# A two-layer post-norm decoder on one core: first scan and constants moved into the schedules, and VectorE steps given to other engines

## The chip, the core and the metric

The kernel runs on one core of a Trainium2 chip. TensorE (PE), VectorE (DVE), ScalarE (ACT) and GpSimd (POOL) each work through their own queue in order; SyncE (SP) issues most of the DMAs, in order too, and GpSimd issues the indirect ones. The metric is device time of one execution in microseconds.

## The reference

A batch of 64 sequences of 128 tokens, width 128, float32, goes through two layers of three blocks; after every block comes `x = layernorm(x + block(x))`.

- Layer 0: a linear attention (`rms_norm`, q/k/v, `exp(k)` with running sums over the tokens, a gated output), a cross-attention with 16 heads of 8 over a context of 77 tokens with a bias and a mask, and a mixture of experts (two shared ones, and the best 2 of 8 for each token).
- Layer 1: a selective scan, `h = exp(delta*A)*h + delta*u*B; y = h.C + u*D`, with 16 states for each of 256 channels, behind a causal convolution of width 4; a cross-attention with 16 heads of 64; and a feed-forward block with ternary weights and activations rounded to 8 bits:

```python
def _bitlinear(x, w):
    return jnp.einsum('bsi,oi->bso', _act_quant(x), _weight_quant(w))
gate = jax.nn.silu(_bitlinear(x, w_gate))
up = _bitlinear(x, w_up)
return _bitlinear(gate * up, w_down)
```

## The kernel before, in words

**Tiling.** The sequences are cut into 16 groups (`g`) of four (`b`). A tile of one group is 128 partitions by 4 x 128 floats. Routed experts work on chunks (`ch`) of two groups: their rows are sent by GpSimd with indirect DMAs into a buffer in DRAM (`rows_in`, zeroed beforehand by `c_fill`, L845 to L857), sorted by expert, worked on in 15 tiles of 256 rows (`c_tile`) and fetched back with indirect DMAs (`c_get`, L417, mixed into the residual at L406).

**Order of the work.** Each layer is one hand-written schedule, the class `Flow` (from L67). Threads (Python generators) yield steps; a step names its engine, a cost, what it depends on and the buffer slots it takes. `Flow.run` takes, again and again, the step that can start first by these costs, with `ahead` as a handicap or bonus for a thread, `table` for ScalarE's function table (a switch is counted as 1.3 us) and `port` for steps that must not overlap with one another on the port which DVE and POOL share. The outcome is a fixed order of instructions in each engine's queue; `Wait` only orders the plan, and on the chip an instruction waits for the data and the buffers it uses. `flow.run(16)` plans layer 0 with up to 16 groups open, `flow.run(5)` layer 1 with five. Expert tiles of the last four chunks are placed in layer 1, beside the scan.

**Layer 0** (L433 to L1069). Per group: `a_head`, `a_seq`, `a_tail` (linear attention), `b_load`, `b_head`, `b_seq`, `b_tail` (cross-attention; the row-maximum subtraction L785 runs on POOL; `b_load` adds the mask to the bias on POOL at L684), `c_route`, `c_rank`, `c_send`, `c_shared`. Weights that belong to layer 1 are collected in `later` by `reserve` and loaded through SP by the thread `weights(later)`, added at group 4; x is loaded group by group at L543, and fills are issued as soon as x of an early group was requested.

**Layer norm** (`norm`, L255 to L279). For each sequence of the group DVE runs `bn_stats` and `bn_aggr` (L261, L262); POOL then turns mean and variance into scale and shift in four small instructions (L269 to L272); ACT applies them (L278). There are seven norms per group (lnA, lnB, lnC, ln1 to ln4). The first block's `rms` (L527 to L536) uses `bn_aggr` too.

**Between the layers** (L1070 to L1145). Layer 0's buffers are given back. Then, outside of any schedule: `negA`, the convolution's taps (loaded and multiplied by `W_in`), its edge and bias constants, the four weights `yWq`, `yWk`, `yWv`, `yWo` of the cross-attention and its folded output bias, and the ternary weights of the feed-forward block. Only then does `Flow` plan layer 1.

**Layer 1.** `scan_inputs(g)` (L1205 to L1300): load x from DRAM (`mid`), transpose, the convolution (L1230, with its edge at L1233), Silu on ACT, the projection (L1253), which goes to DRAM (`rows`) to be broadcast, and delta = softplus(...) on PE (L1268), ACT (abs at L1278), DVE (maximum at L1282, a correction at L1294) and three POOL passes (L1297 to L1299). `spread(g)` fetches the rows of B and C, broadcast over the partitions, two states at a time; `decays(g)` computes dA on ACT (L1359); `states(g)` multiplies du and B on DVE (L1375) and runs the scan on DVE (L1383); `outputs(g)` multiplies h and C on POOL (L1407) and sums over states on PE with identity matmuls into `acc` (L1420). A group has 16 such steps. Then come `gates`, ln1, the cross-attention (`cross_inputs`, `values`, `attend`), ln2, ln3, and `feed(g)`, which rounds the activations, multiplies by the ternary weights and forms `silu(gate)*up` with a Tanh on ACT (L1758) and two DVE steps (L1762, L1766), then a scale per row (L1772 to L1774), a rounding on DVE (L1777) and ACT (L1783), and the product with the last weights (L1799).

## Time and profile before

| | |
|---|---|
| runs, us | 3307.13, 3314.45, 3314.62 |
| profiled execution, us | 3323.51 |
| its span, us | 3321.7 |
| granted TensorE clock, mean | 0.941 |
| PE busy | 2867.3 us, 86% |
| DVE busy | 2616.4 us, 79% |
| ACT busy | 2097.9 us, 63% |
| POOL busy | 1741.2 us, 52% |
| DMA | 438.23 MB, mean 132 GB/s |

The span reaches from the first to the last instruction of the profiled execution; device time has 1.8 us around it. "Busy" is the time in which an engine works on an instruction of its own. A group of the profile is all instructions of one line with one shape: line, engine, operation, output <- inputs, shapes, count, then busy us and mean ns, and idle time of the engine ahead of them with what ended most of it. Line numbers in the views of this kernel are those of the listing above.

### The profile page before, as it was taken

To read this page: it belongs to the slowest core of one execution; us is meant where nothing else is said; L and a number is where in the kernel's file an instruction comes from. 1 tells how busy PE (TensorE), PEld (TensorE's weight loads), DVE (VectorE), ACT (ScalarE), POOL (GpSimd) and SP (SyncE) were. 2 spreads that over 40 slices of the span, in tenths; PEclk is the share of its full clock that TensorE was granted. 3 is DMA by queue.
4 is the path that set the end of the run, shared out by engine and by line. 5 is a ranking of instruction groups with operands and counts; after the bars stand their busy time and mean duration, and the time that the engine had idled before them with its cause. 6 is when DMAs were issued, how large, how long until landed. Compare 5 with 4: busy or idle time off the path is not lost. (4 is left out here: it accounts for less than half of the span.)

```text
span 3321.7 us, 55836 instructions
## 1 busy us (share of the span) xinstructions
PE 2867.3 (86%) x19880; PEld 1937.7 (58%) x19880; DVE 2616.4 (79%) x5007; ACT 2097.9 (63%) x3831; POOL 1741.2 (52%) x1603
## 2 busy tenths in 40 slices
PE   3989999999996679889898988888899988888883
PEld 2667777776864346556464655555665655656462
DVE  3777787888754488878987888888888898879864
ACT  1655767667731566767666766666677767767653
POOL 3454564655454356445745556664645556554531
PEclk7899999999998899999998999999999999999986
DMA  5134252333223464365545554464536533333400
GB/s 152 46 95 123 71 142 71 108 105 85 67 82 117 140 232 151 128 189 172 188 149 179 178 180 166 147 213 154 173 118 196 173 119 127 116 121 122 154 23 7
DMA packets 256542, 438.23 MB, mean 132 GB/s; under 512 B 40683, under 2 KB 155014, under 8 KB 256262
## 3 DMA queue, kind: packets, MB, share of 16 engines
q1 hardware_dynamic: 248070, 417.86, 39.9%
q0 software_dynamic: 8192, 16.79, 1.6%
q8 instruction: 157, 2.57, 0.3%
q14 instruction: 123, 1.01, 0.1%
HBM read 376.37 MB, written 58.20 MB: 131 GB/s over the span
## 5 line engine op out<-in xcount | busy, mean ns | idle before, releaser
L1407 POOL TENSOR_TENSOR h<-h,C 128x1024 f32<-128x1024 f32 x256 | 604.6, 2363 | 571.4 <-DVE bu L1375 365.5
L1420 PE MATMUL acc<-h,ident 128*128 128x512 f32 x1024 | 540.1, 653 | 138.5 <-POOL h L1407 137.5
L1383 DVE TENSOR_TENSOR_SCAN h<-dA,bu 128x1024 f32<-128x1024 f32 x256 | 583.8, 2280 | 26.7 <-PE acc L1420 7.7
L1375 DVE TENSOR_TENSOR bu<-du,B 128x1024 f32<-128x1024 f32 x256 | 355.8, 1390 | 79.2 <-DMA B<-rows 77.2
L1420 PEld LDWEIGHTS acc<-h,ident 128*128 128x128 f32 x1024 | 187.2, 201 | 346.5 <-POOL h L1407 193.5
L1359 ACT ACTIVATE dA<-delta,negA 128x508 f32<-128x508 f32 x512 | 336.4, 714 | 57.2 <-DVE h L1383 56.7
L349 PE MATMUL mm<-t_rT,t_we 128*128 128x256 f32 x960 | 250.8, 394 | 14.9 <-DMA t_we<-in_we 6.7
L1609 POOL TENSOR_TENSOR s<-s,rs 128x1232 f32<-128x1232 f32 x64 | 145.6, 2276 | 175.7 <-DVE rs L1603 111.6
L349 PEld LDWEIGHTS mm<-t_rT,t_we 128*128 128x128 f32 x960 | 175.9, 194 | 76.5 <-issue 22.6
L785 POOL TENSOR_TENSOR s<-s,mx 128x1232 f32<-128x1232 f32 x64 | 144.0, 2255 | 143.9 <-DVE mx L782 69.5
L1509 PE MATMUL mm<-xT,w_yWq 128*128 128x256 f32 x512 | 165.6, 406 | 21.4 <-ACT kT L1502 8.9
L1627 ACT COPY pT<-mm 77x512 f32<-77x512 f32 x256 | 136.4, 583 | 55.9 <-PE mm L1616 53.9
L1498 ACT ACTIVATE qT<-mm,w_ybq 128x256 f32<-128x256 f32 x256 | 122.4, 478 | 68.7 <-PE mm L1510 67.8
L793 ACT COPY pT<-mm 77x512 f32<-77x512 f32 x256 | 132.7, 586 | 50.8 <-PE mm L800 45.1
L1566 PEld LDWEIGHTS mm<-kT,qT 64*128 64x128 f32 x2048 | 130.3, 194 | 51.3 <-issue 18.6
L1616 PE MATMUL mm<-ident,s 128*77 128x128 f32 x1024 | 140.9, 283 | 19.7 <-POOL s L1609 10.6
L977 POOL DMA_INDIRECT rows_in<-cx,pos x128 | 124.3, 971 | 57.9 <-DVE pos L957 24.9
L800 PE MATMUL mm<-ident,s 128*77 128x128 f32 x1024 | 139.3, 290 | 17.1 <-ACT s L787 12.4
L417 POOL DMA_INDIRECT t_got<-rows_out,pos x128 | 131.2, 1025 | 40.6 <-issue 28.5
L1616 PEld LDWEIGHTS mm<-ident,s 128*77 128x77 f32 x1024 | 118.9, 152 | 54.8 <-POOL s L1609 21.8
L1566 PE MATMUL mm<-kT,qT 64*128 64x77 f32 x2048 | 148.0, 286 | 0.9 <-DVE s L1592 0.4
L374 PEld LDWEIGHTS mm<-t_we,t_th 128*128 128x128 f32 x960 | 123.6, 197 | 32.8 <-issue 15.1
(335 smaller groups left out, 7025.5 us busy)
## 6 DMA issues: line engine op xcount, KB each, us to landing
B<-rows SPq DMA_DIRECT2D x256, 512.0 KB, 4.9
C<-rows SPq DMA_DIRECT2D x256, 512.0 KB, 4.0
t_we<-in_we SPq DMA_DIRECT2D x120, 384.0 KB, 3.6
rows_in<-zero SPq DMA_DIRECT2D x8, 1920.0 KB
t_row<-rows_in SPq DMA_DIRECT2D x120, 128.0 KB, 3.2
rows_out<-t_yo SPq DMA_DIRECT2D x120, 128.0 KB, 3.6
cg<-in_ctxT SPq DMA_DIRECT2D x32, 154.0 KB, 4.4
x<-in_x SPq DMA_DIRECT2D x16, 256.0 KB, 4.2
```

The lines of the kernel that those rows point to most:

```text
L349: mm(o[:, c * TR : (c + 1) * TR], we.tile[:, n * 256 + c * P : n * 256 + (c + 1) * P], rT.tile, start=True, stop=True,)
L785: lambda: pool.tensor_tensor(s, s, mx.tile.unsqueeze(2).to_broadcast([P, NH, M]), ALU.subtract), port=True,
L800: nc.tensor.transpose(pt[0:M, i * P : (i + 1) * P], s[:, 4 * q + i, :], ident)
L1359: act(dA[:, j, :, 1:], delta[:, c, :, 1:], AF.Exp, scale=negA[:, c, n + j : n + j + 1])
L1375: order[g, c, n] = dve.tensor_tensor(bu, du[:, c, :].unsqueeze(1).to_broadcast([P, 2, W]), BC["B", g, c, n], ALU.mult)
L1383: dve.tensor_tensor_scan(h.rearrange("p n s -> p (n s)"), DA[g, c, n].rearrange("p n b s -> p (n b s)"), bu.tile.rearrange("p n s -> p (n ...
L1407: one = pool.tensor_tensor(h, h, BC["C", g, c, n], ALU.mult)
L1420: mm(acc, ident, HS[g, c, n][:, j, :], start=n + j == 0, stop=n + j == NS - 1)
L1509: mm(pk[:, 0 : 2 * P], yWq[:, cs], xT.tile[:, pair * 2 * P : (pair + 1) * 2 * P], start=True, stop=True)
L1566: mm(sc[:, i * M : (i + 1) * M], qT[r, i, b2 * P : (b2 + 1) * P], kT[r, i, b2 * M : (b2 + 1) * M], start=True, stop=True,)
L1609: lambda: pool.tensor_tensor(s, s, rs.tile.unsqueeze(2).to_broadcast([P, NH, M]), ALU.mult), port=True,
L1616: nc.tensor.transpose(pt[0:M, i * P : (i + 1) * P], s[:, 4 * q + i, :], ident)
```

## The change

The diff, cut to what acts; `...` marks what is left out. The line numbers of the changed kernel differ from those above.

In the common part, ahead of layer 0, room is made that outlives layer 0, and `norm` skips `bn_aggr`, whose work POOL does from the two halves that `bn_stats` gives:

```diff
+    magic = new(const, [P, 1], "magic")
+    pool.memset(magic, MAGIC)
...
+    negA, conv_all = new(const, [P, 2, NS], "negA"), new(const, [P, 2], "conv_all")
+    taps, first = new(const, [P, 4, 256], "taps"), new(const, [3, 256], "first")
+
+    iT0 = new(const, [P, G, P + 3], "iT0")
+    pool.memset(iT0[:, :, 0:3], 0.0)
+    u0, delta0, du0 = (new(const, [P, 2, W], n) for n in ("u0", "delta0", "du0"))
+    sl_rows = Slots([new(dram, [3 * NS, W], f"rows{i}", bufs=1) for i in range(2)])
...
-            dve.bn_stats(st[:, b, :], v[:, b, :])
-            dve.bn_aggr(mv[:, b, :], st[:, b, :])
...
-            yield flow.dve(0.55, key + ("st", b), deps, lambda: stats(b))
+            yield flow.dve(0.3, key + ("st", b), deps, lambda: dve.bn_stats(st[:, b, :], v[:, b, :]))
...
-            pool.tensor_scalar(r, mv[:, :, 1], LN_EPS, None, ALU.add)
-            pool.tensor_scalar(sh, mv[:, :, 0], -1.0, None, ALU.mult)
+            pool.tensor_tensor(d, st[:, :, 1], st[:, :, 4], ALU.subtract)
+            pool.tensor_tensor(r, st[:, :, 2], st[:, :, 5], ALU.add)
+            pool.tensor_tensor(sh, st[:, :, 1], st[:, :, 4], ALU.add)
+            pool.tensor_tensor(d, d, d, ALU.mult)
+            pool.tensor_scalar(r, r, 1.0 / P, LN_EPS, ALU.mult, ALU.add)
+            pool.tensor_scalar(d, d, 0.25, None, ALU.mult)
+            pool.tensor_scalar(sh, sh, -0.5, None, ALU.mult)
+            pool.tensor_tensor(r, r, d, ALU.add)
             pool.tensor_tensor(r, r, mhalf[:, :G], ALU.pow)
             pool.tensor_tensor(sh, sh, r, ALU.mult)
-        yield flow.pool(2.0, key + ("r",), [key + ("st", b) for b in range(G)], steps)
+        yield flow.pool(3.3, key + ("r",), [key + ("st", b) for b in range(G)], steps)
```

Indirect DMAs are planned as users of the shared port, and a mix waits, in the plan, for both loads of its pair:

```diff
-            yield S.flow.dve(0.7, k + ("mix", b), [k + ("got", b), k + ("v",)], add)
+            yield S.flow.dve(0.7, k + ("mix", b), [k + ("got", b | 1), k + ("v",)], add)
...
-            (got,) = yield S.flow.pool(2.0, k + ("got", b), out, get, S.got, landing=3.0)
+            (got,) = yield S.flow.pool(2.0, k + ("got", b), out, get, S.got, landing=3.0, port=True)
...
-                yield POOL(1.0, ("send", g, b, i), [...], send, landing=3.0)
+                yield POOL(1.0, ("send", g, b, i), [...], send, landing=3.0, port=True)
```

In layer 0: x of group 0 is loaded second; fills and `later` wait for a first layer norm in the plan; slots are fewer; the scan's constants and `scan_inputs(0)` (the same steps as before, with the maximum on ACT) are threads of layer 0:

```diff
     w_qkv = load(w0, "w_qkv", [P, 384])
+    x0 = new(w0, [P, G, P], "x0")
+    nc.sync.dma_start(out=x0, in_=tokens(t["x"], 0))
     w_swiglu = load(w0, "w_swiglu", [P, 256])
...
-        sl_y = slots(3, p, [P, G, P], "y")
+        sl_y = slots(2, p, [P, G, P], "y")
-        sl_s = slots(4, p, [P, NH, M], "s")
+        sl_s = slots(3, p, [P, NH, M], "s")
-        sl_pT = slots(6, p, [M, 4, P], "pT")
+        sl_pT = slots(4, p, [M, 4, P], "pT")
-        sl_a = slots(4, p, [P, W], "a")
+        sl_a = slots(3, p, [P, W], "a")
-        sl_sum = slots(2, p, [P, G, P], "sum")
+        sl_sum = slots(1, p, [P, G, P], "sum")
-        S = Experts(..., **tile_slots(p, 2, 2, 2, 2, 2, 1, 3))
+        S = Experts(..., **tile_slots(p, 2, 2, 2, 2, 2, 1, 2))
...
-            yield Wait([("a", min(NG - 1, 1 * ch + 1), "x")])
+            yield Wait([("lnA", CH * ch, 0)])
             yield SP(("fill", ch), [], fill)
...
-        flow.add(4, weights(later))
+        flow.add(1, weights(later, ("lnA", 1, 0)))
...
+        flow.add(2, scan_constants(flow, sl_eh, sl_T))
+        flow.add(13, scan_inputs(0, E), ahead=-0.5)
...
-                yield DVE(
-                    0.75, k + ("max", c), [k + ("dt", c), k + ("abs", c)],
-                    lambda: dve.tensor_scalar(delta.tile[:, c, :], pz.tile, bias, 0.0, ALU.add, ALU.max),
-                )
+            yield ACT(
+                0.7, k + ("max", c), [], lambda: act(delta.tile[:, c, :], pz.tile, AF.Relu, bias=bias)
+            )
```

`scan_constants` loads half of `W_in` and the convolution's rows through SP (into tiles of layer 0's slots `T` and `eh`), clears a tile on POOL, and forms `taps`, `first`, `conv_all` and `negA` on DVE and ACT, as the code between the layers did. In layer 1, everything between the layers is gone; the constants of the cross-attention and of the feed-forward block are two threads, and their users wait for them in the plan:

```diff
+        def cross_constants():
+            k = ("k", "y")
+            for n, w in (("yWq", yWq), ("yWk", yWk), ("yWv", yWv), ("yWo", yWo)):
+                yield SP(k + (n,), [], lambda: nc.sync.dma_start(out=w, in_=t[n]))
...
+        def feed_constants():
...
+                (w,) = yield SP(k + (n,), [], lambda o: nc.sync.dma_start(out=o, in_=t[n]), sl_fh)
...
+        flow.add(0, cross_constants(), feed_constants(), ahead=-0.5)
...
-            yield Wait(normed(("ln1", g)))
+            yield Wait(normed(("ln1", g)) + y_ready)
...
-            yield Wait(normed(("ln3", g)))
+            yield Wait(normed(("ln3", g)) + [("k", "f", "tern", i) for i in range(3)])
...
-                    0.7, k + ("tanh", b), [k + ("up", b)],
-                    lambda: act(h, pg.tile, AF.Tanh, scale=sg[:, b : b + 1]), table="exp",
-                )
-                yield DVE(
-                    0.7, k + ("g", b), [k + ("tanh", b)],
-                    lambda: dve.scalar_tensor_tensor(h, h, 1.0, pg.tile, ALU.add, ALU.mult),
+                    0.7, k + ("g", b), [k + ("up", b)],
+                    lambda: act(h, pg.tile, AF.Silu, scale=sg[:, b : b + 1]), table="silu",
                 )
...
-                def scaled():
-                    dve.tensor_scalar(h, h, w["hs"], MAGIC, ALU.mult, ALU.add)
...
-                yield DVE(0.45, k + ("scaled", b), [], scaled, port=True)
+                yield ACT(
+                    0.75, k + ("scaled", b), [k + ("scale", b)],
+                    lambda: act(h, h, AF.Identity, scale=w["hs"], bias=magic),
+                )
...
         for g in range(NG):
-            flow.add(g, scan_inputs(g), ahead=0.25)
-            flow.add(g, gates(g), residual(g), ahead=0.0)
+            if g:
+                flow.add(g, scan_inputs(g, E), ahead=0.25)
+            flow.add(g, gates(g), residual(g), ahead=0.5)
```

In the order of SP's queue that results, the 24 loads ahead of the mask of group 1 are the weights of layer 0, x of groups 0 to 4, bias of groups 0 to 2, the mask of group 0, the shared experts' weights and cg of group 0; the first fill and the `later` weights follow cg of group 2. In layer 1, 17 instructions of SP stand ahead of the first load of B. ScalarE's queue has 203 table loads, and had 190.

## Prediction

> **What bounds the kernel now.** The order of reading: busy time by stage, the timeline at the two places where TensorE is empty, the waits inside layer 1, and the groups that the change removes. Columns of the first view: stretch in us, its length, busy us of PE, PEld, DVE, ACT and POOL with instruction counts, granted clock, DMA share, GB/s.
>
> ```profile
> 0.00:56.00 56.00, 9.29 (x22) 5.35 (x22) 11.82 (x51) 4.84 (x8) 11.56 (x38) 0.81 0.81 225
> ...
> 100.00:1040.00 940.00, 897.87 (x8497) 674.87 (x8497) 722.36 (x1922) 582.46 (x1141) 501.59 (x698) 0.97 0.33 91
> ...
> 1055.00:1119.00 64.00, 36.23 (x106) 18.07 (x106) 18.18 (x40) 25.92 (x33) 7.92 (x8) 0.74 0.38 127
> 1119.00:3190.00 2071.00, 1811.66 (x10514) 1159.46 (x10516) 1759.30 (x2660) 1401.01 (x2471) 1156.52 (x758) 0.96 0.49 159
> 3190.00:3322.00 132.00, 76.11 (x598) 55.97 (x592) 66.95 (x208) 62.01 (x125) 29.33 (x39) 0.75 0.02 5
> ```
>
> Five stages with five limits: a start in which PE has 9.29 of 56 us and the DMA engines 81%; layer 0 with PE at 897.87 of 940 (96%, 42 us idle); an empty passage; layer 1 with PE at 87% and DVE at 85%, neither alone the bound; a tail of 132 us. The timeline gives the cause of the two holes:
>
> ```profile
> 52.69 0.83 POOL L684 TENSOR_TENSOR bias<-bias,mask 128x308 f32<-128x308 f32 x1 [33.23 <-DMA mask<-in_mask]
> ...
> 1055.14 0.16 DVE L1093 TENSOR_REDUCE conv_all<-w_conv_w 128x2 f32<-128x8 f32 x1 [9.87 <-DMA rows_in<-cx,pos]
> ...
> 1118.90 2.29 DVE L1383 TENSOR_TENSOR_SCAN h<-dA,bu 128x1024 f32<-128x1024 f32 x1
> ```
>
> GpSimd stands 33.23 us before the mask of group 1, which lies in SP's queue behind three zero fills (1.97 MB each), the `later` weights and x; the `rms` steps behind it in POOL's queue are what DVE, and through it PE, waits for. Layer 0 lets go of its buffers at 1055.14, with the last sent rows, and the first scan starts at 1118.90: 63.8 us of constants, x loads and the first `scan_inputs`. Inside layer 1 (total us, times, longest):
>
> ```profile
> PE acc L1420 <- POOL h L1407: 137.5, 107, 6.2
> ```
>
> ```profile
> DVE bu L1375 <- DMA B<-rows: 77.2, 47, 6.8
> ```
>
> PE's largest wait is for the product h*C, which waits for DVE. So time taken from DVE reaches PE only in part, and GpSimd lies on that way.
>
> **The change part by part**, against the profiled execution, 3323.5 us (span 3321.7). The median of the runs is 3314.45, 9.1 less; the sum is carried over to it.
>
> *Start: -32.* x of group 0 becomes SP's second load, and fills and `later` weights stand behind the loads of the first groups. Ahead of the mask of group 1 now stand 24 loads of 4.0 MB together, with no fill. At the 225 GB/s of the first stretch that is 17.8 us, with landing about 20; 24 issues of 0.47 us (12 us) fit under it. GpSimd goes on at 20 instead of 52.7. Fill 0 and the weights then move while nobody waits. What is late next: SP stops at the scan constants (their half tile, and a memset that POOL does after the second lnA), with bias, mask and cg of group 3 queued behind; POOL needs that mask only after four row-maximum subtractions, where it already waited 0.40 us, so I charge nothing here. Ends: 0 (the hole only moves) and -36.
>
> *Layer 0: +12.* `scan_inputs(0)` moves in. On PE, by the groups of its lines over 16 executions: L1230 7.5, L1233 0.8, L1253 1.9, L1268 2.2, four transposes 0.6: 13 us. PE is 96% busy here, so nothing hides it: +12. Its ACT work (about 8 us) and three POOL passes (2.42 + 2.46 + 2.52 = 7.4) lie beside PE; the POOL passes stand between the last softmax subtraction and the last lnB, where POOL waits for attention anyway. Uncovered, they would cost 7.4. The constants add 2 us of DVE and 6 loads.
>
> *Layer 0 with fewer buffers: +8.* s goes 4 to 3, pT 6 to 4, y 3 to 2, a 4 to 3, sum 2 to 1, got 3 to 2. No row shows the effect: ends are -5 and a doubling of the 42 us that PE idles. I take the near end, since a few waits are all there is now. The three norms here lose 192 `bn_aggr` on DVE, not the bound, and add 48 x 1.7 = 82 us to POOL (502 of 940 busy), hidden under PE.
>
> *Passage: -40, and +5.* After the release SP issues 17 instructions before the first B load: four x, tile rows and weights, two cg, the four yW: 4.0 MB and the 0.5 of B itself. At 216 GB/s (the stretch 1060 to 1080) that is 21 us, then one `bu` of 1.22: the first scan about 23.5 us after the release instead of 63.8. Ends -25 and -46. PE's 36 us in the old passage were useful work; 13 are booked above, the rest falls into the new passage but for about 5.
>
> *Layer 1, DVE relief: -60.* The rows that go (busy us, mean ns | idle):
>
> ```profile
> L1762 DVE SCALAR_TENSOR_TENSOR fh<-fh,mm 128x512 f32<-128x512 f32 x56 | 37.4, 669 | 2.7 <-ACT fh L1758 2.5
> L1777 DVE TENSOR_SCALAR fh<-fh,q 128x512 f32<-128x512 f32 x56 | 28.6, 511 | 0.0
> L1282 DVE TENSOR_SCALAR delta<-mm,w_dt_bias 128x512 f32<-128x512 f32 x28 | 20.7, 738 | 15.1 <-ACT h L1278 15.1
> L406 DVE SCALAR_TENSOR_TENSOR t_v<-t_got,gate,t_v 128x128 f32<-128x128 f32 x64 | 51.9, 818 | 3.5 <-ACT x L278 1.1 <-DMA t_got<-rows_out,pos 0.9 <-DMA t_v<-mid 0.5
> L262 DVE BATCH_NORM_AGGREGATE ln1mv<-ln1st 128x2 f32<-128x6 f32 x60 | 10.9, 182 | 2.1
> ```
>
> One `silu` in place of tanh and a product takes L1762: 37. The rounding L1777 goes to ACT: 29. The maximum L1282 becomes a Relu on ACT: 21. `bn_aggr` in five norms: 260 of them, where a pair takes 0.42 and `bn_stats` alone 0.29: 0.13 each, 34. L406 has a median of 351 and a mean of 818 (up to 5274) and is now planned away from GpSimd's indirect loads: up to 64 x 0.47 = 30; half, 15. Together 136 to 151 of 1759. Ends: nothing, and all but what PE's own work stops (-140). PE idles 259 us here and 137.5 of it is that one wait; I take half of 145, -73. Against it: 72 norms, each with ten POOL steps instead of four; the rows show 0.28 to 0.31 from start to start, so 1.7 us a norm, 122 us, with h*C queued behind on POOL and `acc` on PE behind that. POOL is 56% busy; most of it falls into its idle time and I charge 13. ACT gains 64 x 0.72 + 32 x 0.69 and 13 more table loads (203 for 190) of 1.28, 85 us on an engine at 68%: nothing. The new wait for `tern` and yW is met long before.
>
> SBUF — State Buffer, "Who interferes with whom", speaks against moving norms to GpSimd: a DVE operation with two SBUF inputs and a GpSimd operation that reads SBUF exclude each other, and the second waits in full. The trace agrees: the first norm step takes 0.23 us at median in lnA and 1.11 in ln2. By the rule an estimate is one whole `bu` (1.39) per norm, 100 us more on POOL, and the sum would lose most of its -60; by the rows (0.31 more on average over the five norms) it loses 22.
>
> ScalarE: Activation LUTs, "Rules for kernel authors", puts relu and max on VectorE. Here, reading PSUM, ACT's abs takes 685 ns and DVE's maximum 740, so the rule would keep 21 us on DVE and the rows do not.
>
> *Tail: +4.* The last group runs alone: four norms at +1.7 - 0.5 each, one table load 1.3, four quarter feeds at -0.4.
>
> Sum: -32 + 12 + 8 - 40 + 5 - 60 + 4 = **-103**: 3323.5 to 3220.5, in the median 3314.45 to **3211**.
>
> **The rivals.**
> *Relief unpaid.* PE's order and the B loads set layer 1 (77.2 us of waits for B, which a faster DVE meets sooner). For it: PE at 87% while DVE already idles 312 us. Layer 1 gives 0: -43, 3271.
> *Relief paid in full.* DVE is the true limit, PE's idle time being its echo. For it: the 137.5 us. Layer 1 -140: -183, 3131.
> *The change doesn't do what it says ahead of layer 1:* the start's hole comes back at group 3's mask (-10 instead of -32) and fewer buffers cost 42 instead of 8: -47, 3267.
> *Slower:* GpSimd becomes the way that counts. Each of the 72 norms holds up h*C by 1.7 and PE with it: +122 with no relief: +79, 3393. It decides once PE's wait at L1420 for L1407 passes about 137 + 100 us, so that the gains ahead of layer 1 are gone. Against it: POOL's 571 us of idle time before h*C.
>
> **How the numbers follow.** Forecast 0.40, relief unpaid 0.22, paid in full 0.16, ahead of layer 1 0.12, slower 0.10. The forecast's own range, from the ends of start and passage and half the relief, is 3160 to 3260; the asked range reaches to the faster rival and over the two middling ones, 3120 to 3300, and leaves out the slower one. A measurement of this kernel tells 0.3% from no change. Faster 0.87, same 0.03, slower 0.10.
>
> **What would show it.** POOL's first long wait ends near 20 us; the first scan comes some 24 us after the last sent rows; PE in layer 0 stays at 95% or more; DVE's busy time in layer 1 falls by some 145 us and PE's wait for h*C falls below 100. Wrong it is if that wait grows, or if layer 0 idles over 60 us in its body.

## The result, and the profile after

The changed kernel takes **3315.47 us** in the median of 12 runs (3308.01 to 3321.65), the kernel before 3313.97 us beside it (12 runs, 3302.70 to 3323.15): ratio **1.0008, 95% interval 0.9994 to 1.0023**. The forecast was 3211 us. The change makes no difference that these runs can tell; the 103 us of the forecast are missing.

The profiled execution of the changed kernel took 3313.49 us (span 3311.8, 9.9 less than the profiled one before). First the busy time by stage (columns as in the prediction's first view):

```profile
0.00:56.00 56.00, 26.28 (x82) 16.43 (x82) 34.87 (x130) 15.55 (x36) 26.87 (x74) 0.88 0.45 120
...
100.00:1040.00 940.00, 870.76 (x8130) 654.50 (x8129) 673.97 (x1725) 564.96 (x1106) 532.46 (x912) 0.96 0.35 97
1053.00:1073.00 20.00, 11.37 (x30) 5.48 (x30) 2.16 (x6) 5.94 (x9) 1.16 (x4) 0.74 0.84 299
1073.00:3165.00 2092.00, 1820.31 (x10472) 1165.37 (x10496) 1654.43 (x2264) 1491.35 (x2576) 1224.36 (x1146) 0.95 0.48 158
3165.00:3311.80 146.80, 83.98 (x654) 63.71 (x655) 58.52 (x166) 77.98 (x143) 42.11 (x84) 0.78 0.01 4
```

The start is as promised: PE has 26.28 us of the first 56 instead of 9.29. But in the body of layer 0 PE is now idle for 69 us of 940 instead of 42, and layer 1 takes 2092.0 us from its first scan to its last, 36 longer than before (2056.4), although DVE is busy for 1654 us there instead of 1755. The kernel before, from first scan to last:

```profile
1118.90:3175.30 2056.40, 1796.96 (x10410) 1149.26 (x10411) 1754.89 (x2656) 1396.17 (x2462) 1149.81 (x755) 0.96 0.49 160
```

The timeline of GpSimd at the start, and that of VectorE behind layer 0, show the two holes gone:

```profile
20.77 0.83 POOL L836 TENSOR_TENSOR bias<-bias,mask 128x308 f32<-128x308 f32 x1
```

```profile
1071.58 1.23 DVE L1378 TENSOR_TENSOR bu<-du,B 128x1024 f32<-128x1024 f32 x1 [11.62 <-DMA B<-rows]
1072.94 2.29 DVE L1386 TENSOR_TENSOR_SCAN h<-dA,bu 128x1024 f32<-128x1024 f32 x1
```

The mask of group 1 is worked on at 20.77 instead of 52.69, the first scan starts at 1072.94 instead of 1118.90. The last rows of layer 0 are sent at 1053.0, though, and were sent at 1052.6 before. PE's largest wait inside layer 1 (total us, times, longest):

```profile
PE acc L1423 <- POOL h L1410: 142.6, 102, 7.0
```

The wait for h*C should have fallen under 100; it is as large as before (137.5). PE is busy for 2862.9 us in all (2867.3 before), and its idle time mostly moved. Worked out from the windows of both kernels, as length less PE's busy time:

| PE idle, us | before | after |
|---|---|---|
| 0 to 100 | 58.9 | 33.1 |
| 100 to 1040 | 42.1 | 69.2 |
| 1040 to last rows sent | 8.2 | 3.4 |
| last rows sent to first scan | 30.1 | 8.6 |
| first scan to last | 259.4 | 271.7 |
| last scan to end | 55.6 | 62.8 |
| sum | 454.4 | 448.9 |

So the question is where 26 us of the start, 22 us of the passage and VectorE's relief went.

### The profile page after: what moved, and what is told of

Read it like the earlier page. It is cut to its first block, busy times and chain, and to the rows that moved or that the text cites. A ratio compares the mean times of both kernels' runs of the same rounds, so it can differ in the third digit from the quotient of the medians.

```text
span 3311.8 us, 55890 instructions
## 1 busy us (share of the span) xinstructions
PE 2862.9 (86%) x19853; PEld 1939.9 (59%) x19880; DVE 2466.8 (74%) x4383; ACT 2190.5 (66%) x3940; POOL 1866.1 (56%) x2276
## 4 chain that ended last, share of the span: by engine, by line
PE 31%; DVE 16%; POOL 11%; ACT 6%; DMA 5%; issue 4%; SPq 1%; POOLq 0%; DVEq 0%; ACTq 0%
PE acc L1423 8%; POOL h L1410 5%; DVE h L1386 4%; DMA B<-rows 3%; DVE bu L1378 3%; PE mm L504 2%; PE mm L1633 2%; PE mm L1683 2%; PE mm L1703 2%; PE mm L1732 2%; PE mm L1597 2%; POOL rows_in L1129 1%; PE mm L1576 1%; PE mm L361 1%; PE mm L386 1%
## 5 line engine op out<-in xcount | busy, mean ns | idle before, releaser
L1423 PE MATMUL acc<-h,ident 128*128 128x512 f32 x1024 | 546.8, 661 | 143.8 <-POOL h L1410 142.6
L1378 DVE TENSOR_TENSOR bu<-du,B 128x1024 f32<-128x1024 f32 x256 | 364.2, 1423 | 100.9 <-DMA B<-rows 98.4
L937 POOL TENSOR_TENSOR s<-s,mx 128x1232 f32<-128x1232 f32 x64 | 144.7, 2267 | 146.2 <-DVE mx L934 90.2
L952 PE MATMUL mm<-ident,s 128*77 128x128 f32 x1024 | 134.7, 286 | 39.3 <-ACT s L939 36.1
L928 DVE TENSOR_TENSOR s<-mm,bias 128x308 f32<-128x308 f32 x256 | 109.0, 469 | 75.0 <-PE mm L911 74.2
L1655 DVE TENSOR_REDUCE mx<-mm 128x4 f32<-128x308 f32 x256 | 119.7, 467 | 58.6 <-PE mm L1633 57.5
```

What stands on the lines that cost most here:

```text
L937: lambda: pool.tensor_tensor(s, s, mx.tile.unsqueeze(2).to_broadcast([P, NH, M]), ALU.subtract), port=True,
L1378: order[g, c, n] = dve.tensor_tensor(bu, du[:, c, :].unsqueeze(1).to_broadcast([P, 2, W]), BC["B", g, c, n], ALU.mult)
L1423: mm(acc, ident, HS[g, c, n][:, j, :], start=n + j == 0, stop=n + j == NS - 1)
```

## The experiments

Every kernel was timed beside the kernel before on the same chip, and each ratio is to that. In the first twelve experiments of the table, on three chips, before took 3421 to 3429 us; in the last six, on two others, 3308 to 3314. Most of the added 110 us lie in layer 0 there (the changed kernel sends its last rows at 1138 instead of 1053); its layer 1 is 24 us longer (2116 instead of 2092). In the twelve, VectorE stands in the first 1195 us for 42 to 114 us in waits of over 3 us that the profile puts to no work of this kernel; in the profiles of the six and of the two kernels themselves there is no such wait. In `after_again` the longest, 19.5 us to 477.6, lies beside a batch of 16 sends on GpSimd, and in the same time ScalarE waits 19.2 us with nothing that the profile names. What holds the engines there is open, and the sum differs from order to order (75 us in `after_again`, 114 in `a_lag`, 42 in `a_noport`). Stage times are therefore compared only between kernels with the same time of before, and the end of layer 0 in the twelve is not the work of the order alone.

"In its own order" means that the planner saw the same steps, costs and slots, and only what a step issues was changed: every queue keeps its sequence. Where a cost, a slot or a claim changes, the planner draws a new order.

| run | order | ratio to before (95%) | last rows sent | from there to the end |
|---|---|---|---|---|
| after_again | changed kernel's | 0.9987 (0.9966 to 1.0008) | 1138.2 | 2286.6 |
| b_start | new in layer 0 | 0.9935 (0.9912 to 0.9958) | 1130.9 | 2263.0 |
| b_relief | before's | 1.0123 (1.0086 to 1.0160) | 1147.3 | 2303.2 |
| b_norms | before's | 1.0111 (1.0086 to 1.0136) | 1162.9 | 2305.5 |
| b_relief_act | before's | 1.0001 (0.9984 to 1.0017) | 1152.6 | 2267.2 |
| a_slots | new | 1.0020 (1.0002 to 1.0038) | 1141.8 | 2286.3 |
| a_send | new in layer 0 | 1.0002 (0.9980 to 1.0025) | 1164.2 | 2288.3 |
| a_noport | new | 0.9909 (0.9876 to 0.9943) | 1138.5 | 2243.5 |
| a_best1 | new | 1.0118 (1.0096 to 1.0140) | 1190.9 | 2278.4 |
| a_lag | new | 1.0096 (1.0066 to 1.0126) | 1190.1 | 2260.5 |
| a_aggr | changed kernel's | 0.9959 (0.9938 to 0.9981) | 1156.6 | 2271.5 |
| a_pe | changed kernel's | 0.9947 (0.9925 to 0.9969) | 1145.9 | 2258.9 |
| a_pool | changed kernel's | 0.9726 (0.9696 to 0.9757) | 1049.0 | 2169.4 |
| a_dve | changed kernel's | 0.9779 (0.9745 to 0.9812) | 1046.6 | 2189.9 |
| a_np_aggr | a_noport's | 0.9850 (0.9808 to 0.9893) | 1035.0 | 2231.9 |
| b_lag | new | 1.0126 (1.0090 to 1.0162) | 1079.7 | 2267.0 |
| a_fills | changed kernel's | 1.0061 (1.0038 to 1.0083) | 1059.1 | 2258.5 |
| np_fills | a_noport's | 0.9887 (0.9863 to 0.9912) | 1044.8 | 2213.9 |

The last two columns, in us, come from the one profiled execution of each. For `a_send` it was 29 us longer than the median of its runs, for the others it lay within 11 us of it.

### The start

`b_start` is the kernel before with x of group 0 loaded second, fills behind `lnA`, the `later` weights at group 1 (the diff's own hunks). Its layer 1 keeps before's plan.

```diff
+    x0 = new(w0, [P, G, P], "x0")
+    nc.sync.dma_start(out=x0, in_=tokens(t["x"], 0))
...
-            yield Wait([("a", min(NG - 1, 1 * ch + 1), "x")])
+            yield Wait([("lnA", CH * ch, 0)])
...
-        flow.add(4, weights(later))
+        flow.add(1, weights(later, ("lnA", 1, 0)))
```

> The kernel before with the start of the change alone: x of group 0 as the second load, fills behind lnA of their groups in the plan, the later weights at group 1 behind lnA of group 1; slots, norms, constants and layer 1 as before. In the changed kernel the start came 31 us earlier and the last rows of layer 0 were sent at 1053 us all the same. If the other edits of layer 0 took the 31 us back, GpSimd goes on at about 21 us here, the last rows are sent at about 1022, and the time is 3314 - 31 = 3283. If the end of layer 0 is set by something that the start does not reach (GpSimd's sends, which stood back to back from 944 to 1053 in the kernel before), the last rows are sent at about 1050 and the time is 3310 to 3316.

0.9935 is 22 us: most of the 31, less than all. `a_fills` goes the other way, in the changed kernel's own order, and `np_fills` does the same in another order. `early[ch]()` issues the fill of chunk `ch`, and its planned step then issues nothing:

```diff
+            def load_mask(o):
+                if g == 1:
+                    for ch in range(3):
+                        early[ch]()
+                nc.sync.dma_start(out=o, in_=tokens(t["mask"], g))
```

> The changed kernel in its own order, but the first three zero fills (5.9 MB) stand on SP ahead of the mask of group 1 again, as in the kernel before; nothing else moves. At the 225 GB/s of before's start they take 26 us, so GpSimd goes on at some 46 us instead of 21. If the start's gain is still in the changed kernel and something later took as much, layer 0 ends some 25 us later and the time is 1.006 to 1.010 of before. If layer 0's end is held by the order of GpSimd's sends and the last attention, so that the start's gain is lost there, the last rows are sent within 10 us of 1053 and the time is 0.998 to 1.004.

> The same three fills ahead of the mask of group 1, in the order of a_np_aggr (0.985; its last rows are sent at 1035, not 1053, with the same start). If in that order the start's 31 us reach the end of layer 0, the last rows are sent 20 to 26 us later and the time is 0.991 to 0.994. If they do not reach it there either, 0.983 to 0.988, and its earlier end comes from the order alone.

GpSimd's timeline in `a_fills`, with the wait ahead of the instruction in brackets:

```profile
39.34 0.83 POOL L844 TENSOR_TENSOR bias<-bias,mask 128x308 f32<-128x308 f32 x1 [18.30 <-DMA mask<-in_mask]
```

The hole that comes back is 18.6 us (39.34 - 20.77), not 26: from 20.0 to 39.3 the core moved 283 GB/s, and not the 225 that I took. Of these 18.6, 6 to 12.5 us are left where layer 0 ends (1059.1 us; three profiles of the changed kernel's layer 0 beside the same time of before end at 1046.6, 1049.0 and 1053.0), and in time 1.0061 stands against 1.0008, 0.5% or some 18 us. In the order of `a_noport` it is 9.9 us at the end of layer 0 and 0.4%, with intervals that overlap. Between a third of the start's gain and nearly all of it is in the changed kernel. So it was not all lost; something else in layer 0 takes the rest.

### Layer 0: buffers, or the order of the sends?

At its end the changed kernel shows a hole that was not there before. The stretch 950 to 1000, first before, then after:

```profile
950.00:1000.00 50.00, 44.54 (x201) 28.87 (x199) 27.90 (x93) 14.12 (x29) 38.22 (x68) 0.93 0.29 96
```

```profile
950.00:1000.00 50.00, 27.70 (x315) 20.87 (x314) 23.64 (x57) 26.38 (x43) 29.55 (x42) 0.76 0.08 27
```

GpSimd's timeline of the changed kernel says why: the rows of chunk 6 are sent, 32 of them in two batches, before the last four row-maximum subtractions of the cross-attention (L937), for which ScalarE and then PE wait. Below it PE's own wait for them:

```profile
958.98 1.09 POOL L1129 DMA_INDIRECT rows_in<-cx,pos  x1 [4.04 <-DVE pos L1109]
...
978.06 0.96 POOL L1129 DMA_INDIRECT rows_in<-cx,pos  x1 [0.22 <-issue]
979.03 6.66 POOL L937 TENSOR_TENSOR s<-s,mx 128x1232 f32<-128x1232 f32 x3
```

```profile
PE mm L952 <- ACT s L939: 18.4, 1, 18.4
```

Two causes were tried. `a_slots` gives the slots back (`got`, too; `a` stays at 3) and takes `scan_inputs(0)` out of layer 0:

```diff
-        flow.add(13, scan_inputs(0, E), ahead=-0.5)
+        sl_y = slots(3, ...); sl_s = slots(4, ...); sl_pT = slots(6, ...); sl_sum = slots(2, ...)
```

> The changed kernel with the first scan_inputs back in layer 1's schedule and the slots of layer 0 as before (y 3, s 4, pT 6, sum 2, got 3; a stays 3). If too few slots took back the 31 us of the start, the last rows are sent at about 1015 to 1025 instead of 1053, the first scan is about 30 us after that instead of 20, and the time is about 3290. If slots are not it, layer 0 ends at about 1040 (13 us of TensorE less), the first scan is no earlier than 1073, and the time is 3308 to 3325.

1.0020 is no gain: fewer slots are not shown to be the cause. Since the order is a new one, they are not excluded either. `a_send` takes the sends' claim on the shared port out of the plan, `a_noport` that of the fetches, too, and lets a mix depend on its own fetch alone:

```diff
-                yield POOL(1.0, ("send", g, b, i), [...], send, landing=3.0, port=True)
+                yield POOL(1.0, ("send", g, b, i), [...], send, landing=3.0)
-            (got,) = yield S.flow.pool(2.0, k + ("got", b), out, get, S.got, landing=3.0, port=True)
+            (got,) = yield S.flow.pool(2.0, k + ("got", b), out, get, S.got, landing=3.0)
-            yield S.flow.dve(0.7, k + ("mix", b), [k + ("got", b | 1), k + ("v",)], add)
+            yield S.flow.dve(0.7, k + ("mix", b), [k + ("got", b), k + ("v",)], add)
```

> The changed kernel without the claim of the sends on the shared port; fetches and mixes keep theirs, so the plan of layer 1 is the changed kernel's own. If that claim puts 32 sends ahead of the last row-maximum subtractions and costs layer 0 what the empty TensorE from 950 to 1000 showed, the last subtraction ends some 20 to 30 us earlier against the last send, and the time is 0.4 to 0.8% below the changed kernel's. If a_noport's gain came from layer 1's fetches, this stays within 0.3% of it.

> The changed kernel with sends and fetches planned as in the kernel before: no claim on the shared port, and a mix behind its own fetch alone. In the changed kernel 32 sends of 1.26 us stand in GpSimd's queue ahead of the last row-maximum subtractions of layer 0, and TensorE has 27.7 of 50 us from 950 to 1000. If the claim on the port in the plan caused that order, the subtractions go ahead of the sends, the last rows are sent 15 to 30 us earlier and the time is 3285 to 3300. If the order has another cause, layer 0 ends at 1050 again; without the claim layer 1's mixes may run into the loads, up to 15 us: 3313 to 3330.

`a_send` gains nothing (1.0002), but it does not test the hole: in its profile 16 sends still stand ahead of the last four subtractions, and 16 more ahead of the last one. No run took the sends away from there in a kept order, so what the hole costs at the end of layer 0 is open. `a_noport` is faster by 0.8% than the changed kernel (0.9909 against 0.9987), but not where I expected it: layer 0 ends at 1138.5 as in `after_again` (1138.2), and the profile's 43 us are gained behind it.

### Is the order a draw?

`a_lag` and `b_lag` change no work at all, in the changed kernel and in the one before:

```diff
-    LAG = 0.15
+    LAG = 0.16
```

`after_again` is the base of the experiments.

> The changed kernel itself, unaltered, beside the experiments: the base for all that undo a part of it. 1.0008 of before in its own measurement (0.9994 to 1.0023); 0.997 to 1.004 is expected here by every theory. If it comes out below 0.995, the two chips differ in what they make of the change, and a_noport's 0.991 and a_aggr's 0.996 have to be read against that.

> The changed kernel with nothing changed but one constant of the plan: the lag that the planner puts between engines, 0.16 instead of 0.15. No instruction is added, removed or altered, only the order that falls out. If the plan is stable, the time is within 0.3% of the changed kernel. If the order is a draw that no single cost decides, it moves by 0.5% or more either way, and differences of that size between planned variants say nothing of the edit that caused them.

> The kernel before with nothing changed but the planner's lag, 0.16 instead of 0.15. If its order was picked among several and lies at the good end of what such draws give, it is 0.5% or more slower. If before's plan is stable and only the changed kernel's is a draw, within 0.3%.

`after_again` stays where it was. Both others are slower, by 1.1% (1.0096 over 0.9987) and 1.3%. In `a_lag` layer 0 ends 52 us later, of which the unexplained waits of VectorE can be 39 (114 instead of 75), and what follows is 26 us shorter. `b_lag` has no such waits, and its layer 0 ends 27 us later (1079.7 instead of 1052.6): that is the order alone. `a_best1` and `a_np_aggr` go further. Both hold the same instructions: `a_noport` with the norms' work as before. `a_np_aggr` keeps the planned costs of the norms (0.3 and 3.3) and so a_noport's order, `a_best1` plans with 0.55 and 2.0.

> The changed kernel without the claims of sends and fetches on the shared port (as a_noport, which gave 0.991) and with norms as before, in work and in planned cost. If the two prices are separate and add up, 0.978 to 0.985. If they are one and the same wait, about 0.990.

> The order of a_noport (0.991, the best so far) kept, with the work of the norms as before: bn_aggr on VectorE and four GpSimd steps. In the changed kernel's order the same edit gave 0.996 for 0.999. If GpSimd's added steps cost the same in this order, 0.986 to 0.989; if they stand where GpSimd waits anyway, 0.990 to 0.993. a_best1, the same instructions in an order planned anew, gave 1.012: a difference to it is the order alone.

1.0118 and 0.9850: 2.7% between two orders of the same work. The two stand on chips with different times of before, though, and `a_best1` has 104 us of the unexplained waits; behind the last rows sent, the one takes 2278.4 us and the other 2231.9. How much of the 2.7% is the order alone is not shown; the 1.3% of `b_lag` is. The order that falls out of the plan is worth as much as any part of this change, so a difference of 1% between two planned variants does not tell what an edit costs. The next comparisons keep the order.

### Layer 1: what is VectorE's relief worth, and GpSimd's work?

`b_relief` hands over the norms, delta's maximum and the scaling to 8 bits in before's order; `b_norms` does the first of these, `b_relief_act` the other two. The `silu` in one step (37 us of the prediction's 145) and the mixes (15) were not tried alone:

```diff
-            dve.bn_stats(st[:, b, :], v[:, b, :])
-            dve.bn_aggr(mv[:, b, :], st[:, b, :])
+            dve.bn_stats(st[:, b, :], v[:, b, :])
...
-                    dve.tensor_scalar(h, h, w["hs"], MAGIC, ALU.mult, ALU.add)
+                    act(h, h, AF.Identity, scale=w["hs"], bias=magic)
```

> The kernel before with its planned order of every queue kept, and only the work of some steps handed over: norms without the aggregate step on VectorE and with ten GpSimd steps, the maximum of delta as Relu on ScalarE, the scaling to 8 bits on ScalarE; silu stays Tanh and a product. By the rows of before this takes 34 + 29 + 21 = 84 us from VectorE in layer 1. If relief of VectorE is worth half, as the prediction had it, and only the new order of the changed kernel hides that, the time is about 3314 - 42 + 13 = 3285. If relief in an unchanged order is worth nothing because TensorE waits elsewhere, 3308 to 3318. If the added GpSimd steps cost what the rival named, 3330 or more.

> The kernel before in its planned order, with the norms alone as in the change: bn_aggr gone from VectorE, ten GpSimd steps instead of four. b_relief, which hands over this and two steps to ScalarE, was 1.2% slower than before (ratio 1.012). If the GpSimd steps are the price, this is as slow or slower: 1.010 to 1.022. If the price lies in the steps given to ScalarE, 0.997 to 1.004.

> The kernel before in its planned order, with delta's maximum (Relu) and the scaling to 8 bits on ScalarE alone; norms as before. VectorE loses some 50 us by the rows, GpSimd gains nothing. If GpSimd's norm steps were the price of b_relief, this is at or below before: 0.990 to 1.000. If ScalarE's longer chain in feed and in scan_inputs was, 1.006 to 1.014.

Layer 1 from first scan to last in `b_start` (whose layer 1 is before's), `b_relief_act` and `b_norms`, all beside the same time of before:

```profile
1204.00:3251.00 2047.00, 1792.09 (x10424) 1143.81 (x10426) 1747.88 (x2656) 1397.32 (x2464) 1149.56 (x755) 0.96 0.50 161
```

```profile
1226.00:3276.00 2050.00, 1788.54 (x10407) 1144.53 (x10424) 1712.66 (x2572) 1452.78 (x2549) 1146.54 (x755) 0.96 0.50 161
```

```profile
1235.00:3324.00 2089.00, 1808.03 (x10415) 1157.92 (x10430) 1718.87 (x2397) 1399.75 (x2464) 1224.55 (x1145) 0.95 0.49 158
```

In the second, DVE has 35 us less and ACT 55 more: layer 1 is as long as it was. In the third, DVE has 29 us less and POOL 75 more: layer 1 is 42 us longer. So in before's order the relief by these two steps is worth nothing and the norms on GpSimd cost 1.1%. Beside the added steps du*B takes 1411 ns in the mean, where the three profiles of before's order with the old norms (`before`, `b_start`, `b_relief_act`) have 1361 to 1390 (5 to 13 us over 256 of them), and PE's wait for h*C is 145 us instead of 117 to 138; what the 42 are made up of was not separated. `a_aggr` takes them back to VectorE in the changed kernel's own order, which was planned with their cost:

```diff
-            yield flow.dve(0.3, key + ("st", b), deps, lambda: dve.bn_stats(st[:, b, :], v[:, b, :]))
+            yield flow.dve(0.3, key + ("st", b), deps, lambda: stats(b))
...
-            pool.tensor_tensor(d, st[:, :, 1], st[:, :, 4], ALU.subtract)
+            pool.tensor_scalar(r, mv[:, :, 1], LN_EPS, None, ALU.add)
+            pool.tensor_scalar(sh, mv[:, :, 0], -1.0, None, ALU.mult)
```

> The changed kernel in its own planned order, but with the work of the norms as before: bn_aggr on VectorE, four GpSimd steps. The changed kernel stood at 1.0008 of before. If the GpSimd steps cost it what they cost in the order of before, this is some 1.0 to 1.4% faster: 0.985 to 0.993, with GpSimd's busy time 120 us less. If the changed order has made room for them, 0.998 to 1.006.

0.9959 against 0.9987, 0.3% with overlapping intervals; `a_np_aggr` against `a_noport` is 0.6%, likewise, and from different times of before. The sign is the same in three orders; the size, where the order was planned for the GpSimd steps, is a quarter to a half of 1.1% and not sure.

### Layer 1: what holds it?

Three kernels leave out work of one engine each in the changed kernel's own order: `a_pe` 7 of 16 sum products, `a_pool` half of each h*C, `a_dve` half of each du*B.

```diff
-                    for j in range(2):
+                    for j in range(2 if n + 2 == NS else 1):
...
-                    one = pool.tensor_tensor(h, h, BC["C", g, c, n], ALU.mult)
+                    one = pool.tensor_tensor(h[:, 0, :], h[:, 0, :], BC["C", g, c, n][:, 0, :], ALU.mult)
...
-                        bu, du[:, c, :].unsqueeze(1).to_broadcast([P, 2, W]), BC["B", g, c, n], ALU.mult
+                        bu[:, 0:m, :], du[:, c, :].unsqueeze(1).to_broadcast([P, m, W]), BC["B", g, c, n][:, 0:m, :], ALU.mult
```

> The changed kernel with 7 of 16 identity products of the scan's output sum left out (the second state of a pair, but for the last pair); every step still waits for GpSimd's product as before. It takes 7/16 of 546.8 = 239 us of TensorE work out of layer 1 and nothing from another engine. If TensorE's work and order bound layer 1, so that relief of VectorE cannot pay, at least 140 us of it show: 0.930 to 0.958. If the chain VectorE - GpSimd - loads of B bounds it, under 60 us: 0.982 or more.

> The changed kernel in its own order with half of each product h*C left out (the first state of a pair alone is multiplied on GpSimd). GpSimd loses some 300 us in layer 1, all else keeps its work and its order. a_pe took 239 us of sum products from TensorE and moved the time by 0.4%, while TensorE's wait for h*C grew from 143 to 215 us. If the chain through GpSimd is what holds layer 1, this gains 80 us or more against the changed kernel's 0.999: 0.975 or less. If no single engine does, 0.985 to 0.997.

> The changed kernel in its own order with half of each product du*B left out after the first (one state of a pair). VectorE loses some 160 to 180 us in layer 1, and it stands right ahead of the scan. The prediction's step counted half of what leaves VectorE as gained: 0.999 - 85/3425 = 0.974. If VectorE's work pays only where TensorE would have waited for it, as b_relief_act (50 us less, ratio 1.000) says, 0.988 or more.

Layer 1 of `after_again` and of `a_pe`, then each one's group of sum products (count, busy us, mean ns, idle time ahead of them):

```profile
1162.00:3278.00 2116.00, 1830.04 (x10473) 1171.91 (x10497) 1668.12 (x2264) 1491.66 (x2576) 1228.90 (x1146) 0.94 0.48 156
```

```profile
1169.00:3258.00 2089.00, 1703.44 (x10037) 1127.06 (x10057) 1658.78 (x2265) 1488.83 (x2578) 1225.57 (x1146) 0.90 0.48 159
```

```profile
L1423 PE MATMUL acc<-h,ident 128*128 128x512 f32 x1024 | 546.2, 660 | 144.0 <-POOL h L1410 143.0
```

```profile
L1423 PE MATMUL acc<-h,ident 128*128 128x512 f32 x576 | 357.9, 717 | 216.4 <-POOL h L1410 215.7
```

PE loses 188 us of sum products and is busy for only 127 us less: its other work takes 62 us longer (1284 to 1346, 4.8%), as the granted clock falls from 0.94 to 0.90. Layer 1 is 27 us shorter; 73 us come back as wait for h*C (143 to 216). PE's work alone does not hold layer 1. Now `a_pool` and `a_dve` (to be set against the changed kernel's 2092 us, with 1654 of DVE and 1224 of POOL):

```profile
1069.50:3072.00 2002.50, 1783.30 (x10470) 1152.83 (x10494) 1616.63 (x2263) 1489.58 (x2576) 941.41 (x1145) 0.96 0.52 165
```

```profile
1066.40:3088.60 2022.20, 1790.18 (x10467) 1153.39 (x10490) 1516.41 (x2264) 1488.28 (x2575) 1183.31 (x1146) 0.95 0.52 164
```

POOL has 283 us less and layer 1 is 89 us shorter; DVE has 138 less (I expected 160 to 180) and layer 1 is 70 shorter. Per microsecond taken away: 0.32 for the product h*C on POOL, 0.51 for du*B on DVE, 0.21 for PE's busy time, and nothing for VectorE's steps in `b_relief_act`. The first two are not one engine's alone: in `a_pool` DVE is busy for 38 us less, too (du*B 1346 ns instead of 1423), and in `a_dve` POOL for 41 less. Work on the chain B load, du*B, scan, h*C, sum pays; the two other steps of VectorE that were tried don't. The scan's own queue shows how that can be, ahead of the first scan of group 8 in the changed kernel. Its du is ready on GpSimd at 2003.2:

```profile
2000.83 2.36 POOL L572 TENSOR_TENSOR du<-delta,u 128x1024 f32<-128x1024 f32 x1
```

VectorE's timeline from there, and all engines in these 23.6 us:

```profile
2007.36 1.22 DVE L1378 TENSOR_TENSOR bu<-du,B 128x1024 f32<-128x1024 f32 x1
2012.10 0.29 DVE L1739 TENSOR_TENSOR xb<-xb,mm 128x128 f32<-128x128 f32 x1 [3.52 <-PE mm L1732]
2020.22 0.29 DVE L1739 TENSOR_TENSOR xb<-xb,mm 128x128 f32<-128x128 f32 x1 [7.83 <-PE mm L1732]
2021.58 1.44 DVE L1669 TENSOR_REDUCE rs<-s 128x16 f32<-128x1232 f32 x1 [1.07 <-ACT s L1666]
...
2025.05 1.86 DVE L418 SCALAR_TENSOR_TENSOR t_v<-t_got,gate,t_v 128x128 f32<-128x128 f32 x4 [1.75 <-DMA t_v<-mid]
2026.82 2.28 DVE L1386 TENSOR_TENSOR_SCAN h<-dA,bu 128x1024 f32<-128x1024 f32 x1
```

```profile
2003.20:2026.80 23.60, 22.19 (x176) 16.36 (x174) 9.19 (x21) 18.19 (x36) 15.75 (x28) 1.00 0.47 153
```

Its du*B is done at 2008.6 and the scan runs at 2026.8. In between VectorE stands idle for 14.2 us, 12.4 of them in front of attention steps that wait for PE and ScalarE, and ScalarE, in its own order, makes the first dA only at 2023.5. PE is 94% busy meanwhile, VectorE 39%. No scan ran from 1936 to 2027. Here layer 1 alternates: stretches of attention and feed-forward work, where PE and ScalarE set the pace and VectorE waits, and stretches of scans, where PE waits for VectorE and GpSimd. In a stretch of the first kind a shorter VectorE step is a longer wait; how many of the norms, roundings and maxima stand there was not counted. The stretches belong to the new plan: from the start of one scan to the next the kernel before has at most 25.6 us and `b_lag` at most 27.0; the changed kernel has 93, 42 and 96 us in groups 7, 11 and 13.

The changed kernel's own progress says the same of its relief. Its lead over before at the first scan of a group: 46 us at group 0, 115 at group 6, 44 at group 8, 36 at group 12, and 6 behind at group 14. The two large losses are two such stretches, in groups 7 and 13. Whether another order would keep the 115 is not settled by that: `a_np_aggr`, the fastest, has pauses of the kind, too (52 us in group 6, 129 in group 9). Nor is it known which edit brought them: the change also raises `ahead` of `gates` and `residual` from 0.0 to 0.5, and no run took that back.

## Why the prediction was wrong, step by step

**Start, -32.** The mechanism and its place were right (20.77; I said near 20). Its worth at the end was too high: `b_start` shows 22 us, `a_fills` and `np_fills` a third to nearly all of the 18.6 that they put back.

**Layer 0, +12 and +8.** PE's idle time in the body grew by 27 us, more than the 8 I put down, and past the 60 us that I named as a sign of being wrong. My cause, slots, is not shown (`a_slots`). What the trace shows is an order at the end in which 32 sends go ahead of the last subtractions, with 17 of the 27 us in that place; what it costs at the end of layer 0 is not shown. `b_lag` shows that this end moves by 27 us with the order alone. Start and body together made -12 in my sum and 0 in the profile.

**Passage, -40 and +5.** The first scan comes 19.9 us after the last sent rows (I said 23.5), 46 earlier. But PE had worked 36 of the old 66 us, and its idle time there fell by 22, not 40. From the last rows to the end my sum had -91, the profile has -10 (2269.1 to 2258.8).

**Layer 1, DVE relief, -60: this is the step that failed.** "I take half of 145, -73. Against it: 72 norms ... I charge 13." Half is about right for work on the scan's own chain (`a_dve`, 0.51), and I gave it to work that is not on it. There, in before's order, 35 us of relief are worth nothing (`b_relief_act`), and GpSimd's norm steps cost not 13 but 42 us for 75 of busy time (`b_norms`). Both errors lean the same way: in before's order these steps together cost 1.2% (`b_relief`). The relief itself was too large as well: in the changed kernel VectorE's busy time in layer 1 fell by 100 us, not 145; the mixes gave 7.7 of 15, and du*B took 8.5 longer. In the changed kernel's own order, planned with the new costs, layer 1 is 36 us longer from first scan to last than before; there the norms on GpSimd account for 0.3% and not surely (`a_aggr`), and the rest, with the new pauses between scans, is not shown by a single edit.

The row that should have told me was PE's 137.5 us of wait for h*C. I read it as a debt of VectorE as a whole; by `a_dve` and `a_pool` it is more a debt of the chain. The rival "relief unpaid" (3271) had the right worth for the steps tried, but its reason, PE's order and the loads of B, was not tested apart (`a_pe` takes away work of PE and keeps its order); the "slower" one had GpSimd's price in kind, and a third of its size was measured. That a new order by itself might be better or worse by 1% was in none of my cases, and it is about as large as the gains of start and passage together.

On the SBUF rule of the Trainium skill that I weighed (SBUF — State Buffer, "Who interferes with whom"), by which I estimated 100 us more on GpSimd: the norms added 75 us to its busy time in layer 1, 1.0 per norm, where I had 122 by the rows and my estimate from the page would have had 100 more on top. The rows were nearer, and still too high. Of the five norms of layer 1 only ln2 had the 1.11 us that I read as agreement with the rule; the medians of the first step in the other four were 0.23, as in lnA. VectorE's side, which neither sum had, is small: du*B took 5 to 13 us longer beside the added steps in before's order, and in the changed kernel's order as long with them as without (1412 ns in `after_again`, 1413 in `a_aggr`).

**Tail, +4.** 146.8 us from the last scan instead of 146.4, so +0.4.

`a_np_aggr` beats both kernels: 3266.67 us, ratio 0.9850 (0.9808 to 0.9893). It keeps start, passage and the steps given to ScalarE, has the norms on VectorE, and an order that was planned without the claims on the port.

```profile
1054.70:3062.60 2007.90, 1771.20 (x9982) 1129.83 (x10000) 1624.61 (x2395) 1433.97 (x2472) 1120.24 (x732) 0.94 0.51 164
3062.60:3266.90 204.30, 138.95 (x1146) 104.83 (x1150) 105.70 (x322) 130.37 (x243) 54.59 (x65) 0.82 0.03 10
```

Its layer 1 has 1120 us of POOL where the changed kernel has 1224, and 37 us less than before from the last rows to the end (2231.9 against 2269.1); the last scan comes earlier and more work is left behind it (204 us). How much of that is luck of the order is open: `a_best1` holds the same instructions and is 1.2% slower than before, on a chip with the unexplained waits in layer 0.

## What to carry to other kernels

Relief of a busy engine paid here for work on the chain that others wait for, and not for two steps beside it: before counting a share of it, ask what stands in that engine's queue next, and whether it was waiting there already. Work moved to an engine that is 56% busy need not be free: here it cost 42 us of layer 1 for 75 us of work. Where a planner turns costs into a fixed order, measure the scatter of its orders first, with a change that alters no work (here 1.1 and 1.3%), and test single edits in a kept order.

## What the runs showed of the hardware that was not expected

Taking 188 us of matmul time out of layer 1 lowered the granted clock from 0.94 to 0.90, and PE's other work there took 4.8% longer, so that its busy time fell by 127 us only. (The remaining sum products went from 660 to 717 ns on average, more than the clock's 4%; why is open.) The Trainium skill's page TensorE: Matmul & The Clock Gate, "Part 1: The HAM clock gate (the 'warmup' mystery)", says that the clock follows how busy TensorE has been; the rows agree, with PE at 86% and at 82% of layer 1. A cut of its work was here partly paid back as slower work.

With half of GpSimd's h*C left out, VectorE's du*B, unchanged in work and order, took 1346 ns in the mean (`a_pool`), where it takes 1412 to 1423 beside the whole product (`after`, `after_again`).

Three zero fills (5.9 MB) held up the mask behind them by 18.6 us; in that stretch the core moved 283 GB/s (`a_fills`, 20.0 to 39.3), where the first 56 us of the kernel before had shown 225 on average.
